# Cross-attention on one core: product 1 completed ahead of a sum, product 5's sums in another buffer, and the last batch's product 1 in seven blocks

## The chip, the core and the metric

The kernel runs on one core of a Trainium2 chip. A core has TensorE (PE in the profile, with its weight loads as PEld), VectorE (DVE), ScalarE (ACT), GpSimd (POOL) and SyncE (SP), which run their own instruction streams in order and wait for each other by semaphores; DMA queues are issued from SP and POOL. Matmuls read SBUF and write PSUM, which has eight banks of 512 fp32 columns on 128 partitions. The metric is the device time of one execution in microseconds (us).

## The reference

For each of 8 batches, x1 and x2 are 512 x 1024 (channels x positions), all in fp32:

```python
q = einsum('bcn,dc->bnd', x1, Wq) + bq          # d = 64
k = einsum('bcn,dc->bdn', x2, Wk) + bk[:, None]
v = einsum('bcn,dc->bdn', x2, Wv) + bv[:, None]
attn = softmax(einsum('bnd,bdm->bnm', q, k), axis=2)
out = einsum('bcm,bnm->bcn', v, attn) + x1
```

The kernel computes Y = x2 . attn^T first (512 x 1024 x 1024) and then Wv . Y (512 x 512 x 1024), adds bv and x1, and divides by the softmax's sums in between.

## The kernel before, in words

**Products.** Both large products are done by Winograd's form of Strassen's method: the left matrix, the right matrix and the result are cut into 2 x 2 quadrants, and seven products of quadrants (numbered 1 to 7 in the order in which the table MULT names them) with sums before and after replace eight. "S1" to "S4" are sums of left quadrants, "T1" to "T4" of right ones. The first stage (`first`, stage "y") makes Y from a quadrant of x2 (`s.a`) and of the exponentials (`s.t`); the second (`second`, stage "o") makes the result from Wv (`w`) and Y (`s.y`). Batches are called 0 to 7.

**Seven blocks inside a product.** Most products of the first stage, and some of the second, use the same method once more inside: `left_stream` and `right_stream` make the four left and the three right inner sums on DVE (L522; L537, L542, L544), and `multiply_seeded` runs seven blocks of 256 columns. A running sum ("chain") and one more ("third") sit in PSUM tiles of their own; ACT copies the chain into the quarters of the result's two banks between the steps (L651). The steps come in the order 1, 7, 6, 2, 5, 4, 3. `complete` adds the third part, kept in SBUF as v, to the second bank at the end, on DVE (L666). `multiply_57` (second stage, products 5 and 7) and `multiply_41` (first stage's product 4 interleaved with the second stage's product 1, "o1") are written out by hand. A product without inner blocks is `multiply` (L463), or `multiply_o1` (L483) for the second stage's product 1.

**Banks.** Two pairs of PSUM banks, a0 a1 and c0 c1, hold results; four more buffers are passed round (`ps_s`). In the last batch `o_bank` swaps the roles of a and c in the second stage.

**Order.** The order of all work is written out by hand in `period(s, n, nn, nnn)`: the first stage of batch s, the second stage of s, and between them the scores, maxima and exponentials of the next batch n, the queries and keys of the one after, and the loads. On each engine instructions run in the order in which this function issues them. `s.six` holds for batches 2 to 5, where product 6 has inner blocks too; `s.one` for batches 1 to 6, where product 1 of the second stage has (`five` in `period` means the same); n is None in the last batch.

**Around the change.** `sum_e` makes T1 and T2 (L340) and `sum_t3` has a POOL DMA add a quadrant to T3. `sums_5` are product 5's inner sums; the right ones stand in two buffers, in batches 2 to 5 "u5" and "u1". "u5" also holds, in the second stage, product 5's partial sums and then a block of the result (`uo`), to which a POOL DMA adds x1 and which an SP DMA then writes out. "aI3" holds product 2's inner left sums (batches 2 to 5), later product 3's. `total_1` sums the exponentials over a column: DVE folds (L283, L267), a partition reduction on POOL (L292), and a DMA that spreads one row over the partitions ("few", L294); `invert` takes the reciprocal (L300) and sends it to DRAM ("row", L302), `spread` brings it back on all partitions ("den", L307). `scale_y` multiplies a quadrant of Y with it (L755). `join_67` (L738), `evict_y`, `evict_t3` (L748) and `sum_y` (L427, L429) make the quadrants of Y and their sums.

**The last batch before.** Order after product 1: T1 and T2, complete 1, product 5's sums, product 7's left sums, product 2, then `total_1`, complete 2, y11, the first reciprocal, product 6, S4 (L108), product 7's right and 3's left sums, product 5, the second reciprocal, product 3's right sums, products 7 and 3, product 4's left sums, join, y22, product 4's right sums, product 4 (`multiply_seeded`, in the banks a0 a1), the scalings of y11, T3 and y22, T2 of Y, y21, T1, the scaling of y21, T4, and product 7's right sums of the second stage. The second stage then starts with product 1 as eight matmul instructions of 512 columns (an fp32 matmul shows as two), followed by 6, 2, 5 with 7 and 3, and 4 in `finish`.

Of the kernel before, what the change touches and what calls it, by code (L numbers as in the profile page):

```python
# [15 lines left out]
def kernel(  # L16
# [427 lines left out]
    def o_bank(s, bank):  # L444
        return {"a": "c", "c": "a"}.get(bank, bank) if s.b == B - 1 else bank

    def multiply(s, stage, i, left, right, n_k, hook=None, rows=range(2)):
# [4 lines left out]
        if stage == "o":  # L452
            bank = o_bank(s, bank)
            if i == 2:
                bank, opens = "c" if s.one else "p", False
        for j in rows:
            if opens:
# [20 lines left out]
    def multiply_o1(s):  # L478

        for j in range(2):  # L480
            s.bank["p", j] = ps = ps_s.tile([P, H], F32, tag="s", name=f"ps_o1{j}_{s.b}")
            for k in range(2):
                nc.tensor.matmul(  # L483
                    ps, w["11"][:, k, ts(j, P)], s.y["11"][:, k, :], start=k == 0, stop=False, skip_group_check=True
                )
# [39 lines left out]
    def inner_left(s, i, x, tag):  # L525
        weave(left_stream(s, i, x, tag))
# [105 lines left out]
    def multiply_seeded(s, i, v_tag, hooks={}, bank=None):  # L632
# [40 lines left out]
    )  # L673
    LAST41 = (
        (4, 1), (4, 7), (4, 6), (4, 2), ("o1", 7), ("o1", 1), (4, 5), ("o1", 6),
        ("o1", 2), ("o1", 4), ("o1", 5), (4, 4), ("o1", 3), (4, 3),
    )

    def multiply_41(s):

        s.inner["o1"] = inner_w["o1"]
        chain, third, *four = (
            ps_s.tile([P, H], F32, tag="s", name=f"ps_i4{k}_{s.b}") for k in ("chain", "third", "b0", "b1")
        )
        c, a = (
            [ps_a.tile([P, H], F32, tag=f"{k}{j}", name=f"ps_o{k}{j}_{s.b}_1") for j in range(2)] for k in "ca"
        )
        for j in range(2):
            s.bank["four", j], s.bank["c", j], s.bank["a", j] = four[j], c[j], a[j]
        v = sb.tile([P, 2, H], F32, tag="r", name=f"v41_{s.b}")  # L690
        v4, v1 = v[:, 0, left], v[:, 1, left]
        chain, third, copy = chain[:, left], third[:, left], nc.scalar.copy
        c0, c1, f0, f1 = ([x[:, left], x[:, right]] for x in (*c, *four))
        steps = {
            (4, 1): (chain, True, [(f0[0], chain)]),
            (4, 7): (third, True, [(v4, third)]),
            (4, 6): (chain, False, [(f1[0], chain)]),
            (4, 2): (f0[0], False, []),
            (4, 5): (chain, False, [(f0[1], chain)]),
            (4, 4): (f1[0], False, [(f1[1], chain)]),  # L700
            (4, 3): (f0[1], False, []),
# [12 lines left out]

        for i, z in LAST41 if s.b == B - 2 else ORDER41:
            ps, opens, copies = steps[i, z]
# [13 lines left out]
            if (i, z) == ("o1", 3):  # L730
# [3 lines left out]
                yield  # L734
        complete(four[1], v4)

# [51 lines left out]
    def evict_o(s, k, hook=None):  # L788


        bank, add = RESULT[k] if k != "11" else ("c" if s.one else "p", None)
        bank = o_bank(s, bank)
        r, h = int(k[0]) - 1, int(k[1]) - 1
# [208 lines left out]
    def period(s, n, nn, nnn):  # L1002
# [127 lines left out]
        else:  # L1130
            complete_1 = multiply_seeded(s, 1, "y11", {4: lambda: copied_s4(s)} if s.six else {})
            if s.b == 1:
                complete_1()
            early = s.b > 1 and n is not None
            sum_e(s, *(("T2",) if early else ("T1", "T2")))
            if s.b > 1:
                complete_1()
            sums_5 = (
                left_stream(s, 5, s.a["S1"], "i2"),
                right_stream(s, 5, s.t["T1"], "u5" if s.six else "y21", "u1"),  # L1140
            )
# [85 lines left out]
            if n is None:  # L1227
                inner_left(s, 4, s.a["22"], "a12")
            join_67(s)
# [44 lines left out]
        else:  # L1274
            if late:
                scale_y(s, "11", "T3", "22")
            sum_y(s, "T2")
# [5 lines left out]
        if five:  # L1283
# [5 lines left out]
            if nn is None:  # L1289
                first_sum()  # L1290
                begin_s1(n)
                end_s1(n)
        else:
            multiply_seeded(s, 4, "r", hooks, "c" if n else "a")()
        if n:
            load_a(n, "12")
        if nn:
            load_a(nn, "21", "22")
        evict_y(s, "21")
        if n is None:  # L1300
            sum_y(s, "T1")
        scale_y(s, "21")
        if five:
# [137 lines left out]
```

## Time and profile before

| what | value |
|---|---|
| median of 3 runs | 669.47 us (668.42 to 675.08) |
| the profiled execution's own time | 668.5 us |
| its span, first to last instruction | 666.7 us |
| TensorE busy | 661.5 us, 99% |
| VectorE busy | 617.5 us, 93% |
| ScalarE busy | 372.6 us, 56% |
| GpSimd busy | 225.2 us, 34% |
| granted TensorE clock | 1.0 throughout |
| DMA | 134.8 MB, mean 202 GB/s |

How rows are read: "500.46 3.60 PE L463 MATMUL out<-in ... x8 [0.15 <-DVE y]" in the order of time means start, duration of the merged instructions, engine, line, operation, tiles by name (buffer numbers left out), count, and the idle time of the engine before it with what ended it. In the groups a row has, behind the bar, busy time and mean duration in ns, then idle time. A wait's row has the total, the number and the longest. Consecutive records of one engine may overlap by 0.08 us (DVE) or more (PE), since an instruction starts while the one before still drains. The times of the trace are those of one execution: batch 1 begins at some 117 us, batch 7 at some 596 us, and one batch between takes 80 to 81 us.

### The profile page before, as it was taken

To read this page: it belongs to the slowest core of one execution; us is meant where nothing else is said; L and a number is where in the kernel's file an instruction comes from. 1 tells how busy PE (TensorE), PEld (TensorE's weight loads), DVE (VectorE), ACT (ScalarE), POOL (GpSimd) and SP (SyncE) were. 2 spreads that over 40 slices of the span, in tenths; PEclk is the share of its full clock that TensorE was granted. 3 is DMA by queue.
4 is the path that set the end of the run, shared out by engine and by line. 5 is a ranking of instruction groups with operands and counts; after the bars stand their busy time and mean duration, and the time that the engine had idled before them with its cause. 6 is when DMAs were issued, how large, how long until landed. Compare 5 with 4: busy or idle time off the path is not lost.

```text
span 666.7 us, 7925 instructions
## 1 busy us (share of the span) xinstructions
PE 661.5 (99%) x2618; PEld 431.0 (65%) x2618; DVE 617.5 (93%) x857; ACT 372.6 (56%) x706; POOL 225.2 (34%) x196
## 2 busy tenths in 40 slices
PE   9999999999999999999999999999999999999997
PEld 5434754757658666677666786576865757666864
DVE  0989999999999899998999899998999999998995
ACT  2755467446574564755756647656566455574321
POOL 0125315531255412553124531265214541244400
PEclk9999999999999999999999999999999999999999
DMA  9768677996899969999599995899947994399413
GB/s 307 276 206 296 147 232 139 187 233 220 240 182 220 241 175 283 172 228 245 158 278 186 256 236 152 247 203 234 269 91 171 209 278 132 74 179 250 90 42 125
DMA packets 51961, 134.81 MB, mean 202 GB/s; under 512 B 5712, under 2 KB 8272, under 8 KB 51920
## 3 DMA queue, kind: packets, MB, share of 16 engines
q0 software_dynamic: 24480, 61.94, 50.4%
q1 hardware_dynamic: 27152, 72.10, 30.4%
q8 instruction: 21, 0.34, 0.2%
q10 hardware_dynamic: 288, 0.26, 0.1%
q14 instruction: 20, 0.16, 0.1%
HBM read 86.77 MB, written 16.81 MB: 155 GB/s over the span
## 4 chain that ended last, share of the span: by engine, by line
PE 75%; DVE 16%; DMA 6%; issue 2%; ACT 0%; POOL 0%; ACTq 0%; DVEq 0%; SPq 0%; POOLq 0%
PE ps_yc L555 7%; PE ps_oc L463 6%; PE ps_ya L555 5%; PE ps_oa L598 5%; PE ps_s L237 5%; PE ps_ya L463 4%; PE ps_oa L463 4%; DMA out_dram<-uo 3%; PE ps_q L192 3%; PE ps_i5chain L555 3%; PE ps_i3chain L555 2%; PE ps_i7chain L555 2%; PE ps_k L192 2%; DVE max L257 2%; DMA uo<-in_x_dram 2%
## 5 line engine op out<-in xcount | busy, mean ns | idle before, releaser
L331 ACT ACTIVATE e<-e 128x1024 f32<-128x1024 f32 x60 | 63.4, 1058 | 30.0 <-DVE e L322 28.9
L292 POOL PARTITION_ALL_REDUCE den<-sum x16 | 52.8, 3298 | 69.6 <-DVE sum L267 64.7
L322 DVE TENSOR_TENSOR e<-e,top 128x1024 f32<-128x1024 f32 x60 | 72.6, 1218 | 2.0 <-POOL top L273 2.0
L273 POOL PARTITION_ALL_REDUCE top<-max x16 | 30.0, 1878 | 103.7 <-DVE max L267 85.2
L853 POOL DMA_DIRECT2D sum<-e x21 | 25.6, 1219 | 100.9 <-ACT e L331 45.7
L246 ACT COPY e<-ps_s 128x512 f32<-128x512 f32 x92 | 48.9, 619 | 9.6 <-PE ps_s L237 7.0
L237 PE MATMUL ps_s<-q,k 64*128 64x512 f32 (+1 forms) x192 | 48.0, 601 | 0.0
L257 DVE TENSOR_TENSOR max<-max,e 128x1024 f32<-128x1024 f32 x30 | 36.6, 1219 | 0.2
L237 PEld LDWEIGHTS ps_s<-q,k 64*128 64x128 f32 x192 | 17.4, 186 | 20.9 <-issue 17.4
L307 POOL DMA_DIRECT2D den<-row x16 | 8.9, 558 | 61.7 <-DMA row<-few 45.3
L755 DVE TENSOR_TENSOR y<-y,den 128x1024 f32<-128x1024 f32 x24 | 29.2, 1221 | 0.4
L463 PE MATMUL ps_oa<-yT,w_S 128*128 128x512 f32 x64 | 28.8, 593 | 0.0
L463 PE MATMUL ps_oc<-yT,w 128*128 128x512 f32 x64 | 28.8, 592 | 0.0
L651 ACT COPY ps_yc<-ps_i7chain 128x256 f32<-128x256 f32 x32 | 11.4, 357 | 30.2 <-PE ps_i7chain L555 24.2
L522 DVE TENSOR_TENSOR aI<-a,aI 128x256 f32<-128x256 f32 x60 | 25.2, 420 | 0.6
L522 DVE TENSOR_TENSOR aI<-a 128x256 f32<-128x256 f32 x60 | 25.8, 450 | 0.0
L192 PE MATMUL ps_q<-x_in_x_dram,wqk_sb 128*64 128x512 f32 x112 | 25.6, 598 | 0.0
L651 ACT COPY ps_ya<-ps_i5chain 128x256 f32<-128x256 f32 x32 | 11.4, 357 | 25.1 <-PE ps_i5chain L555 20.9
L340 DVE TENSOR_TENSOR eT<-eT,e 128x1024 f32<-128x1024 f32 (+1 forms) x18 | 24.0, 1365 | 0.1
L651 ACT COPY ps_ya<-ps_i1chain 128x256 f32<-128x256 f32 x28 | 10.0, 357 | 24.6 <-PE ps_i1chain L555 20.9
L555 PE MATMUL ps_yc<-e,aI 128*128 128x256 f32 x92 | 23.6, 379 | 0.0
L598 PE MATMUL ps_oa<-yT,w_S 128*128 128x512 f32 x48 | 23.5, 592 | 0.0
(322 smaller groups left out, 1826.3 us busy)
## 6 DMA issues: line engine op xcount, KB each, us to landing
x_in_x_dram<-in_x_dram SPq DMA_DIRECT2D x60, 512.0 KB, 8.1
a<-in_x2T_dram SPq DMA_DIRECT2D x32, 512.0 KB, 7.3
sum<-e POOLq DMA_DIRECT2D x21, 512.0 KB, 5.7
aS<-in_x2T_dram POOLq DMA_DIRECT2D x19, 512.0 KB, 9.6
eT<-eT POOLq DMA_DIRECT2D x16, 512.0 KB, 11.7
uo<-in_x_dram POOLq DMA_DIRECT2D x14, 512.0 KB, 10.9
r<-in_x_dram POOLq DMA_DIRECT2D x14, 512.0 KB, 8.8
e<-e POOLq DMA_DIRECT2D x14, 512.0 KB, 9.4
```

Source lines behind the costliest of these rows:

```text
L192: nc.tensor.matmul(ps[r, :], w_sb[:, c, :], s.x[:, c, ts(h, H)], start=(c == 0), stop=(c == CT - 1),)
L237: nc.tensor.matmul(ps[g][:, n], s.k[r, ts(i, P)], s.q[r, ts(h, H)][:, n], start=True, stop=True)
L246: nc.scalar.copy(e[:, g, i, :], ps[g])
L257: nc.vector.tensor_tensor(f, e[:, :, 0, :] if i == 1 else f, e[:, :, i, :], op)
L292: nc.gpsimd.partition_all_reduce(s.den[h], s.mx[h][:, 0, :], P, ReduceOp.add)
L322: nc.vector.tensor_tensor(e, e, top, ALU.subtract)
L331: nc.scalar.activation(e, e, AF.Exp)
L463: nc.tensor.matmul(ps, left[ka][:, k, ts(j, P)], right[kb][:, k, :], start=opens and k == 0, stop=i in (2, 3, 4) and k == n_k - 1, skip_gr ...
L522: nc.vector.tensor_tensor(v[k], v[x], v[y], op)
L555: nc.tensor.matmul(ps, s.inner[i][ka][:, k, :], s.inner[i, "t"][kb][:, k, :], start=opens and k == 0, stop=z in (2, 3, 4) and k == n_k - 1 ...
L598: nc.tensor.matmul(ps, w[ka][:, k, ts(j, P)], s.y[kb][:, k, :], start=False, stop=i == 3 and k == 1, skip_group_check=True,)
L651: nc.scalar.copy(out, of)
```

## The change

1. `complete_1()` stands ahead of `sum_e` in every batch from 1 on; before, only in batch 1 (in the others it came right behind T2, or T1 and T2).
2. The first of the two buffers for product 5's right inner sums is "aI3" in place of "u5" in batches 2 to 5.
3. In the last batch product 1 of the second stage is done in seven blocks too: `s.one` now holds there, `multiply_41` takes the place of `multiply_seeded(4)` and `multiply_o1`, with the banks swapped and an order of its own (ORDER41_7). There product 4 has no tiles for chain and third: the right half of its first bank serves as the chain, the left half takes step 7's result, which ACT copies to v before it copies the chain over it. y21 is evicted from those two tiles, and product 2's result from a0 a1.
4. In the last batch S4 and product 4's inner left sums are issued ahead of `total_1` and complete 2; the scaling of y11 and the three inner right sums of o1 stand ahead of the join, where product 4's left sums stood; y21 is scaled ahead of T1.

```diff
-            self.one = 1 <= b < B - 1
+            self.one = b >= 1
...
     def multiply_o1(s):
...
-            bank = o_bank(s, "a")
-            s.bank[bank, j] = a = ps_a.tile([P, H], F32, tag=f"{bank}{j}", name=f"ps_o{bank}{j}_{s.b}_1")
+            s.bank["a", j] = a = ps_a.tile([P, H], F32, tag=f"a{j}", name=f"ps_oa{j}_{s.b}_1")
...
+    ORDER41_7 = (
+        (4, 1), (4, 7), ("o1", 7), ("o1", 1), (4, 6), ("o1", 6), ("o1", 2),
+        (4, 2), (4, 5), ("o1", 4), ("o1", 5), (4, 4), ("o1", 3), (4, 3),
+    )
...
     def multiply_41(s):
...
+        last = s.b == B - 1
+        *inner, four0, four1 = (
+            ps_s.tile([P, H], F32, tag="s", name=f"ps_i4{k}_{s.b}")
+            for k in (() if last else ("chain", "third")) + ("b0", "b1")
+        )
+        to, grow = "ac" if last else "ca"
...
+        if last:
+            chain = f0[1]
+            steps = {
+                (4, 1): (chain, True, []),
+                (4, 7): (f0[0], False, [(v4, f0[0]), (f0[0], chain)]),
+                (4, 5): (chain, False, [(f1[1], chain)]),
+                (4, 4): (f1[0], False, []),
+            }
...
-        if k == "22" or s.b == B - 1 and k == "21":
+        if k == "22":
             bank, add = "a", 6
...
     def period(s, n, nn, nnn):
...
             complete_1 = multiply_seeded(s, 1, "y11", {4: lambda: copied_s4(s)} if s.six else {})
-            if s.b == 1:
-                complete_1()
             early = s.b > 1 and n is not None
+            complete_1()
             sum_e(s, *(("T2",) if early else ("T1", "T2")))
-            if s.b > 1:
-                complete_1()
             sums_5 = (
                 left_stream(s, 5, s.a["S1"], "i2"),
-                right_stream(s, 5, s.t["T1"], "u5" if s.six else "y21", "u1"),
+                right_stream(s, 5, s.t["T1"], "aI3" if s.six else "y21", "u1"),
             )
...
             if n is None:
                 copy_t4(s)
                 add_t4(s)
+                sum_a(s, "S4")
+                inner_left(s, 4, s.a["22"], "a12")
             if s.b > 1:
                 total_1(s)
             complete_2()
...
-                sum_a(s, "S4")
+                if n:
+                    sum_a(s, "S4")
...
             complete_3 = multiply_seeded(s, 3, "r", hooks, "c")
             if n is None:
-                inner_left(s, 4, s.a["22"], "a12")
+                scale_y(s, "11")
+                inner_right(s, "o1", s.y["11"], "i2")
             join_67(s)
...
-                scale_y(s, "11", "T3", "22")
+                scale_y(s, "T3", "22")
...
+        elif late:
+            weave(multiply_41(s))
         else:
-            multiply_seeded(s, 4, "r", hooks, "c" if n else "a")()
+            multiply_seeded(s, 4, "r", hooks)()
...
         evict_y(s, "21")
+        scale_y(s, "21")
         if n is None:
             sum_y(s, "T1")
-        scale_y(s, "21")
...
-        if not five:
+        if s.b == 0:
             second(1)
```

More of the change, by code (lines that the diff above doesn't have):

```diff
@@ L444, in o_bank @@
     def o_bank(s, bank):
[L445 removed]
+        return {"a": "c", "c": "a"}[bank] if s.b == B - 1 else bank
     def multiply(s, stage, i, left, right, n_k, hook=None, rows=range(2)):
@@ L692, in multiply_41 @@
[L692 to L696, printed above, removed]
+            s.bank["four", j], s.bank[to, j], s.bank[grow, j] = (four0, four1)[j], c[j], a[j]
+        if last:
+            v = sb.tile([P, H], F32, tag="top", name=f"v41_{s.b}", bufs=2)
+        else:
+            v = sb.tile([P, 2, H], F32, tag="r", name=f"v41_{s.b}")[:, 0]
@@ new lines, in multiply_41 @@
+        v4, v1, copy = v[:, left], v[:, right], nc.scalar.copy
+        c0, c1, f0, f1 = ([x[:, left], x[:, right]] for x in (*c, four0, four1))
+        if last:
+            chain = f0[1]
[5 more added lines that the diff above has]
+            }
+        else:
+            chain, third = inner[0][:, left], inner[1][:, left]
+            steps = {
+                (4, 1): (chain, True, [(f0[0], chain)]),
+                (4, 7): (third, True, [(v4, third)]),
+                (4, 5): (chain, False, [(f0[1], chain)]),
+                (4, 4): (f1[0], False, [(f1[1], chain)]),
+            }
```

22 lines of the change are left out of this document (9 added, 13 removed).

## The prediction

> **What bounds the kernel now.** I read the profile's page first, then who TensorE waits for, then its order of time, and last the queues that feed it.
>
> ```profile
> PE 661.5 (99%) x2618; PEld 431.0 (65%) x2618; DVE 617.5 (93%) x857; ACT 372.6 (56%) x706; POOL 225.2 (34%) x196
> PE ps_oc L463 <- DVE y L755: 0.2, 1, 0.2
> 633.33 1.03 PE L555 MATMUL ps_i4chain<-eT,a 128*128 128x256 f32 x4
> 634.19 1.03 PE L555 MATMUL ps_i4third<-eI4eT,aI 128*128 128x256 f32 x4
> 639.37 3.60 PE L483 MATMUL ps_o<-y,w 128*128 128x512 f32 x8
> 642.81 1.02 PE L463 MATMUL ps_oc<-yT,w_S 128*128 128x512 f32 x2
> ```
>
> The first row is the page's; the reader sees one engine without a pause and VectorE (DVE) close behind. The next is one of four rows of TensorE's waits, of which only the warm-up's is longer. Records of matmuls overlap, so their cost is read from start to start: four instructions of 256 columns take 634.19 - 633.33 = 0.86 us, 0.215 each; eight of 512 columns take 642.81 - 639.37 = 3.44 us, 0.43 each. The stream of matmuls is the time, and a change is worth what it takes out of this stream or tears into it. DVE idles little, and it decides where the tears are.
>
> **A. Product 1's third part ahead of T2 (batches 2 to 7).** The order on DVE changes, not the work.
>
> ```profile
> 446.10 3.23 POOL L292 PARTITION_ALL_REDUCE den<-sum  x1 [3.51 <-DVE sum L267]
> 447.24 3.31 DVE L340 TENSOR_TENSOR eT<-eT,e 128x1024 f32<-128x1024 f32 x2
> 450.48 0.69 DVE L666 TENSOR_TENSOR ps_ya<-ps_ya,v 128x512 f32<-128x512 f32 x1
> 605.22 2.35 DVE L340 TENSOR_TENSOR eT<-eT,e 128x1024 f32<-128x1024 f32 x2
> 617.36 3.23 POOL L292 PARTITION_ALL_REDUCE den<-sum  x1 [5.51 <-DVE sum L267]
> 617.77 1.28 DVE L771 TENSOR_TENSOR y<-ps_yc,uy 128x512 f32<-128x512 f32 x2
> 619.05 1.62 DVE L108 TENSOR_TENSOR aS<-a,aS 128x1024 f32<-128x1024 f32 x1
> ```
>
> Two sums of 128x1024 take 2.35 us alone, but 3.31 when they start 1.14 us into a partition reduction on POOL: 0.96 lost. S4, begun 1.69 us into one, takes 1.62 instead of about 1.2: 0.4 lost. Both fit one reading: from some point on, a DVE sum of two SBUF tiles can't begin until 2.1 us after the reduction's start. The eviction of y, which reads PSUM and one SBUF tile, runs inside the same stretch in its usual 1.28. Completing product 1 is of that second kind (PSUM and v). Put first, it fills 0.60 us (451.08, the next start, less 450.48) of a pause that T2 has anyway; T2 ends when it ended, and all of DVE's work behind it starts 0.60 us earlier. If completing is held up too, the order costs and brings nothing. I take 0.60.
>
> The Trainium skill, "SBUF — State Buffer", "Who interferes with whom", says that a DVE instruction with two SBUF inputs contends with a GpSimd one that reads SBUF, and one with at most one SBUF input doesn't; the trace agrees in the 3.31 against the 1.28. Were it not so, A's share would fall out of the sum below. The same section has the loser blocked for the other's whole instruction, where these rows show a release at 2.1 of 3.23 us; the measurement decides.
>
> The completion now waits for the copy of step 4. In the last batch:
>
> ```profile
> 601.60 0.36 ACT L651 COPY ps_ya<-ps_i1chain 128x256 f32<-128x256 f32 x1 [0.51 <-PE ps_ya L555]
> 601.98 3.32 DVE L340 TENSOR_TENSOR eT<-e,e 128x1024 f32<-128x1024 f32 x2
> ```
>
> The copy ends at 601.96, DVE comes at 601.98: no wait to speak of. Behind a wait there T2, the inner sums and product 6's operands would queue.
>
> What 0.60 us are worth to TensorE:
>
> ```profile
> L555 PE MATMUL ps_i6chain<-eI6y,aI 128*128 128x256 f32 x16 | 4.4, 398 | 0.0
> L555 PE MATMUL ps_i6chain<-eI6yT,aI 128*128 128x256 f32 x16 | 4.1, 379 | 0.0
> 292.54 0.41 DVE L522 TENSOR_TENSOR aI<-aS,aI 128x256 f32<-128x256 f32 x1
> 293.06 0.73 PEld L555 LDWEIGHTS ps_i6chain<-eI6y,aI 128*128 128x128 f32 x4 [0.27 <-ACT ps_ya L651]
> 293.09 1.10 PE L555 MATMUL ps_i6chain<-eI6y,aI 128*128 128x256 f32 x4
> ```
>
> Sixteen matmuls of product 6's step 6 (four batches) cover 4.4 us, sixteen of step 5 4.1: about 0.07 us a batch, 1.10 instead of 1.03. The named releaser is a copy; but the left sum ends at 292.95 and the weights load 0.11 later, so DVE is the late one. Half a microsecond earlier removes it: **-0.28**.
>
> **B. Product 5's first sums in another buffer (batches 2 to 5).**
>
> ```profile
> DVE eI5u L537 <- DMA out_dram<-uo: 9.0, 4, 2.8
> 454.20 9.45 DMA out_dram<-uo
> 500.46 3.60 PE L463 MATMUL ps_oa<-yT,w_S 128*128 128x512 f32 x8
> 499.27 0.69 DVE L713 TENSOR_TENSOR ps_oc<-ps_oc,v 128x512 f32<-128x512 f32 x1
> 500.00 0.57 ACT L733 COPY ps_oa<-ps_oc 128x512 f32<-128x512 f32 x1 [0.49 <-DVE ps_oc L713]
> 502.93 1.23 DVE L755 TENSOR_TENSOR y<-y,den 128x1024 f32<-128x1024 f32 x1
> 504.21 1.98 PE L463 MATMUL ps_oc<-y,w 128*128 128x512 f32 x4 [0.15 <-DVE y L755]
> ```
>
> Four times DVE waits for the DMA that writes the last batch's result out of u5, 9.0 us in all. The buffer aI3 is free then: product 2 has finished with it, and its next user, product 3's left sums, comes on DVE after product 5's completion, which needs later steps than the sums in aI3. So no wait takes this one's place at once. Mostly the 9.0 us are DVE's own, not TensorE's. Only batch 5 pays: the chain runs over DVE from that DMA to 504.21. Late DVE completes product 1 of the result late (499.27), ACT's copies queue behind it, product 4 and the scaling of y21 follow, and TensorE starts at 504.21 instead of 500.46 + 3.44 = 503.90; its first four also cover 1.98 instead of 3 x 0.43 + 0.59 = 1.88. Together **-0.41**, and nothing if DVE meets another wait on that way; I take the whole, since 2.8 us are freed and 0.4 needed.
>
> **C. Last batch, product 1 of the result in seven blocks.** Eight matmuls of 512 columns become fourteen of 256: 14 x 0.215 = 3.01 for 3.44, **-0.43**. Four small copies come on ACT, which idles there; one completion of 0.6 us on DVE replaces part of the 1.2 of scaling y11, which moves ahead.
>
> Product 4 now uses the right half of its own first bank as the running sum, so its step 6 waits for two copies after step 7 (ACT, L729), with only two one-row blocks (0.86 us) between.
>
> ```profile
> 635.26 0.37 ACT L651 COPY v<-ps_i4third 128x256 f32<-128x256 f32 x1 [0.51 <-PE ps_i4third L555]
> 571.00 0.36 ACT L729 COPY ps_oc<-ps_oc 128x256 f32<-128x256 f32 x1 [1.31 <-PE ps_oc L720]
> 571.27 0.38 ACT L729 COPY v<-ps_oc 128x256 f32<-128x256 f32 x1
> 568.11 1.13 PE L720 MATMUL ps_i4chain<-eI4eT,aI 128*128 128x256 f32 x4
> ```
>
> Step 7's copy starts at 635.26, a second 0.27 to 0.37 later, and it ends at 635.89 to 635.99; TensorE is there at 635.92, and a torn stream adds 0.10 (1.13 for 1.03). So 0.1 to 0.2; I take **+0.18**.
>
> **D. Last batch, S4 and the sums moved.** S4 and product 4's four left sums (0.75 + 0.88) go ahead of the second column sum. Scaling y11 (1.22) and its three inner sums (0.69 + 0.41 + 0.41 by the rows of their shapes above) stand where the left sums stood.
>
> ```profile
> 628.24 0.75 DVE L522 TENSOR_TENSOR aI<-a 128x256 f32<-128x256 f32 x2
> 612.56 0.88 DVE L522 TENSOR_TENSOR aI<-a,aI 128x256 f32<-128x256 f32 x2
> 615.31 1.23 DVE L283 TENSOR_TENSOR sum<-e 128x1024 f32<-128x1024 f32 x1 [1.86 <-DMA e<-e]
> 626.62 0.36 ACT L651 COPY ps_yc<-ps_i7chain 128x256 f32<-128x256 f32 x1 [0.51 <-PE ps_yc L555]
> 623.96 0.54 POOL L307 DMA_DIRECT2D den<-row  x1 [1.93 <-DMA row<-few]
> DMA to landing us min/median/max: 3.5/3.5/3.5
> 630.17 1.23 DVE L738 TENSOR_TENSOR uy<-uy,uy 128x1024 f32<-128x1024 f32 x1 [0.26 <-ACT uy L743]
> 632.64 1.22 DVE L537 TENSOR_TENSOR eI4eT<-eT 128x1024 f32<-128x1024 f32 x1
> ```
>
> DVE idles 1.86 us ahead of the column sum. With A it arrives there at 612.8 (612.56 + 0.88 - 0.60); S4 (1.14, no reduction beside it) and the left sums (1.6) end at about 615.5, so the column sum is 0.2 us late; without A, 0.8. What hangs on it is a queue: POOL's reduction, the DMA few and, behind them in order, the DMAs that spread the FIRST denominators. Those land at 623.96 + 3.5 = 627.5 now, and nobody wants them until product 4's sums (632.64) are long done; afterwards they land at 627.7, and scaling y11 wants them at 627.6: product 7's last copy ends at 626.98, and its completion takes 0.60. From 627.75 the scaling, inner sums (2.7), the join and y22 (2.47) bring product 4's first right sum to 632.95, and its end, with 1.22, to 634.2. TensorE wants it at 634.19 and needs some 0.1 after a sum's end. **+0.25** (0 to 1.0, the upper end for a sum 0.8 late plus the 0.10), since that lies nearest to the rows with A. After that DVE has 1.22 less to do, and y21 is scaled ahead of T1: I see no wait up to the end.
>
> **Sum:** -0.28 - 0.41 - 0.43 + 0.18 + 0.25 = -0.69 us against the profiled execution's 668.5 us (span 666.7): 667.8. The median of the runs shown is 669.47, 0.97 above that execution, with runs from 668.42 to 675.08; I add 0.4 for such scatter: **668.2 us**.
>
> **Rivals.** *The freed DVE time reaches nobody.* B's wait goes, but the stall of batch 5 stays, as another wait takes its place on the way to 499.27. For it: one lateness of 40 us is rarely one wait's alone; against it: the earlier batches idle before the same completion and pay nothing. -0.28 - 0.43 + 0.43 = -0.28: 668.2, with the scatter 668.6. Chance 0.17.
>
> *Slower: the first denominators land late.* If completing product 1 is held by the reduction like T2, A brings nothing, the column sum of the last batch is 0.8 us late, and scaling y11 blocks DVE ahead of join, y22 and product 4's right sums; TensorE pays one for one from 634.19 on. 0 - 0.41 - 0.43 + 0.18 + 0.95 = +0.29: 668.8, with the scatter 669.2 to 669.8. It turns the sign once the scaling is some 0.9 us later than 627.6 and A's share is gone. For it: a slack of over 5 us becomes none. Against it: y's evictions run beside a reduction undisturbed. Chance 0.18.
>
> *It does all it says and nothing else* (D free, as C's wait): -1.0, 667.5. Chance 0.10; my forecast 0.50. The last 0.05 are for something unseen.
>
> **Range and chances.** The forecast alone covers 667.5 to 669.0. With the free case and its run-to-run tenths the range begins at 667.0; it ends at 670.2, the late denominators at their upper bound (D at 1.0) with the median's 0.97 on top. A measurement here can tell about 1%, 6.7 us, from no change; no case comes near it: same 0.95, faster 0.02, slower 0.03.
>
> **What would show it.** In the changed kernel: no DVE wait for out_dram<-uo; step 6 of product 6 at 1.03; second(2) of batch 5 right behind second(6); L666 of product 1 ahead of L340 at 0.69, T2 ending as before. In the last batch fourteen matmuls of 0.215 for L483's eight, a small PE gap at (4,7), another at (4,6), and the scaling of y11 starting just after the den DMA lands. I am wrong if DVE, not TensorE, has idle time taken from it that turns up as PE gaps elsewhere, or if the sums placed ahead push the column sum back by a microsecond.

## The result, and the profile after

The changed kernel takes 668.01 us (median of 22 runs, 667.31 to 668.49) against 669.16 us for the kernel before in the same comparison (22 runs, 668.42 to 675.08). The ratio is 0.9976, with a 95% interval of 0.9967 to 0.9986; on a second chip it was 0.9977 (0.9968 to 0.9986; 667.74 against 669.44 us). That is no change by the prediction's bound of 1% and a small gain by the interval. Some executions of most kernels here take about 6 us more (the one of them that was profiled, in e2, spent 87.79 us in batch 1, at a granted clock of 0.994 over the execution), which widens several intervals below; there I go by the lengths of the batches.

The page of the changed kernel, its busy times and its chain of work that ended last:

```profile
PE 661.0 (99%) x2624; PEld 432.1 (65%) x2624; DVE 614.8 (92%) x861; ACT 373.4 (56%) x709; POOL 224.9 (34%) x196
PE 97%; DMA 2%; DVE 1%; issue 0%; ACT 0%; ACTq 0%; DVEq 0%
```

The busy times hardly move. The chain does: it runs over TensorE for 97% of the span; before, it was 75%, with DVE 16% and DMA 6%. Who waits for whom, TensorE's rows first, then DVE's (total, times, longest):

```profile
PE ps_ya L464 <- ACT e L317: 0.2, 1, 0.2
```

```profile
DVE ps_ya L666 <- ACT ps_ya L651: 7.7, 7, 1.5
```

TensorE's wait for y21 is gone, and so is the wait of DVE for out_dram<-uo (9.0 us). DVE's largest wait behind the first batch's is now product 5's completion waiting for ScalarE's copies, that is, for TensorE's steps: DVE is ahead.

The length of each batch, from TensorE's first matmul of product 1 to the next batch's (the last one to the start of its last matmul), in us, from the trace of each kernel's profiled execution:

| kernel | 1 | 2 | 3 | 4 | 5 | 6 | 7 |
|---|---|---|---|---|---|---|---|
| before | 81.17 | 80.67 | 80.48 | 80.47 | 80.90 | 75.15 | 66.57 |
| after | 81.16 | 80.53 | 80.35 | 80.34 | 80.35 | 75.15 | 66.48 |
| after, second chip | 81.17 | 80.53 | 80.34 | 80.35 | 80.34 | 75.16 | 66.48 |
| e1 order alone | 81.17 | 80.87 | 80.34 | 80.69 | 81.83 | 76.04 | 66.70 |
| e2 buffer alone | 87.79 | 80.68 | 80.47 | 80.48 | 80.47 | 75.16 | 66.80 |
| e3 last batch alone | 81.17 | 80.78 | 80.47 | 80.66 | 81.54 | 75.15 | 67.38 |
| e4 sums back | 81.17 | 80.53 | 80.35 | 80.34 | 80.35 | 75.15 | 68.58 |
| e8 late sum | 81.17 | 80.52 | 80.35 | 80.34 | 80.35 | 75.41 | 69.81 |
| e6 own tiles | 81.17 | 80.53 | 80.34 | 80.35 | 80.35 | 75.15 | 66.19 |
| e7 other order in 6 | 81.17 | 80.54 | 80.35 | 80.34 | 80.35 | 74.87 | 66.56 |
| e9 own chain | 81.17 | 80.54 | 80.34 | 80.35 | 80.34 | 75.15 | 66.31 |
| e10 the same, other order in 6 | 81.16 | 80.53 | 80.35 | 80.34 | 80.35 | 74.87 | 66.24 |
| e11 old buffer | 81.17 | 80.53 | 80.34 | 80.35 | 80.95 | 75.15 | 66.61 |

From batch 1 on the changed kernel's execution is 1.04 us shorter than that of before (span less the start of batch 1: 549.34 and 548.30): 0.52 in the four batches' 0.13, another 0.42 in batch 5, and 0.09 in batch 7. Its head, up to batch 1, was 0.53 longer: TensorE's wait for the load of x_head ended at 12.06 us, in before's execution at 11.54, and from there on both heads take the same time (105.85 and 105.84). Batch 5 in order of time:

```profile
440.29 1.03 PE L555 MATMUL ps_i1chain<-e,a 128*128 128x256 f32 x4
446.22 3.23 POOL L292 PARTITION_ALL_REDUCE den<-sum  x1 [3.51 <-DVE sum L267]
447.36 0.69 DVE L666 TENSOR_TENSOR ps_ya<-ps_ya,v 128x512 f32<-128x512 f32 x1
447.95 2.71 DVE L340 TENSOR_TENSOR eT<-eT,e 128x1024 f32<-128x1024 f32 x2
450.59 0.41 DVE L522 TENSOR_TENSOR aI<-aS 128x256 f32<-128x256 f32 x1
454.11 1.03 PE L555 MATMUL ps_i6chain<-eI6y,aI 128*128 128x256 f32 x4
460.34 1.22 DVE L537 TENSOR_TENSOR eI5aI<-eT 128x1024 f32<-128x1024 f32 x1
500.45 3.60 PE L464 MATMUL ps_oa<-yT,w_S 128*128 128x512 f32 x8
503.88 1.45 PE L464 MATMUL ps_oc<-y,w 128*128 128x512 f32 x3
```

L666 takes its 0.69 beside the reduction, T2 behind it still ends 4.4 us after the reduction's start (447.95 + 2.71 - 446.22; before 447.24 + 3.31 - 446.10 = 4.45), and the first left sum comes 10.30 us after product 1's start (before 451.08 - 440.17 = 10.91). Step 6 of product 6 runs untorn at 1.03. Product 5's first sum starts at 460.34 without a wait, and the second stage passes from product 6 to 2 at 503.88, 3.43 after 500.45, in the stream's own rhythm. The last batch:

```profile
614.95 1.22 DVE L283 TENSOR_TENSOR sum<-e 128x1024 f32<-128x1024 f32 x1
623.59 0.54 POOL L307 DMA_DIRECT2D den<-row  x1 [1.92 <-DMA row<-few]
627.16 1.22 DVE L776 TENSOR_TENSOR y<-y,den 128x1024 f32<-128x1024 f32 x1
632.40 1.21 DVE L537 TENSOR_TENSOR eI4eT<-eT 128x1024 f32<-128x1024 f32 x1
633.74 1.06 PE L741 MATMUL ps_i4b<-eI4eT,aI 128*128 128x256 f32 x4
634.84 0.37 ACT L750 COPY v<-ps_i4b 128x256 f32<-128x256 f32 x1 [2.27 <-PE ps_i4b L741]
635.24 0.36 ACT L750 COPY ps_i4b<-ps_i4b 128x256 f32<-128x256 f32 x1
635.65 1.13 PE L741 MATMUL ps_i4b<-eI4eT,aI 128*128 128x256 f32 x4
642.23 1.94 PE L464 MATMUL ps_oc<-yT,w_S 128*128 128x512 f32 x4
```

The column sum starts as soon as S4 and the left sums are done, without the 1.86 us of idling ahead of it; the scaling of y11 has its denominators in time; product 4's first right sum ends at 633.61, and (4,7) follows at 633.74 with 0.03 lost (1.06 for 1.03). What costs here are the two copies in a row: (4,6) could start at 635.50 (635.28 for the last matmul ahead of it, and 0.215), and starts at 635.65.

### The profile page after: what moved, and what is told of

Its sections match the earlier page's. It is cut to its first block, busy times and chain, and to the rows that moved or that the text cites. A ratio compares the mean times of both kernels' runs of the same rounds, so it can differ in the third digit from the quotient of the medians.

```text
span 666.2 us, 7951 instructions
## 1 busy us (share of the span) xinstructions
PE 661.0 (99%) x2624; PEld 432.1 (65%) x2624; DVE 614.8 (92%) x861; ACT 373.4 (56%) x709; POOL 224.9 (34%) x196
## 4 chain that ended last, share of the span: by engine, by line
PE 97%; DMA 2%; DVE 1%; issue 0%; ACT 0%; ACTq 0%; DVEq 0%
PE ps_yc L555 9%; PE ps_oc L464 8%; PE ps_ya L555 7%; PE ps_s L237 6%; PE ps_oa L598 6%; PE ps_oa L464 5%; PE ps_ya L464 4%; PE ps_q L192 4%; PE ps_i5chain L555 3%; PE ps_i4b L741 3%; PE ps_k L192 3%; PE ps_i3chain L555 3%; PE ps_i7chain L555 3%; PE ps_oc L741 3%; PE ps_i1chain L555 3%; PE ps_i2chain L555 3%
## 5 line engine op out<-in xcount | busy, mean ns | idle before, releaser
L841 POOL DMA_DIRECT2D r<-in_x_dram x14 | 23.2, 1660 | 0.8 <-issue 0.8
```

## The experiments

**e1, the order alone** (kernel before with part A only).

```diff
-            if s.b == 1:
-                complete_1()
             early = s.b > 1 and n is not None
+            complete_1()
             sum_e(s, *(("T2",) if early else ("T1", "T2")))
-            if s.b > 1:
-                complete_1()
```

> The kernel before, with product 1 completed ahead of T2 in batches 2 to 7 and nothing else. Theory (the completion fits into a pause that the partition reduction makes anyway, so DVE is 0.6 us ahead): step 6 of product 6 starts without a gap in batches 2 to 5, each of these batches 0.13 us shorter from product 1 to product 1 as in the changed kernel, about -0.5 us in all; the gap of 0.42 us in batch 5 ahead of y21's product stays. Rival (the late sums come from DVE's wait for the output DMA): the step 6 gaps stay, no change of the time.

Measured: 668.74 us (12 runs) against 669.50, ratio 1.0 (0.9975 to 1.0025): undecided. Batch 3 is 0.14 shorter and step 6 of product 6 is untorn in all of batches 2 to 5. But batches 2, 4 and 5 are longer than before, by 0.2, 0.2 and 0.9. Its order of time in batch 5, then a row of batch 6, and last the row of the DMA issues of batch 5's place (KB, us to landing):

```profile
440.10 1.03 PE L555 MATMUL ps_i1chain<-e,a 128*128 128x256 f32 x4
464.61 1.23 DVE L537 TENSOR_TENSOR eI5u<-eT 128x1024 f32<-128x1024 f32 x1 [4.37 <-DMA out_dram<-uo]
505.07 2.41 PE L463 MATMUL ps_oc<-y,w 128*128 128x512 f32 x5 [0.21 <-DVE y L755]
559.94 1.23 DVE L755 TENSOR_TENSOR y<-y,den 128x1024 f32<-128x1024 f32 x1 [1.19 <-DMA den<-row]
```

```profile
out_dram<-uo SPq DMA_DIRECT2D x1, 512.0 KB, 10.5
```

In this execution the write of uo took 10.5 us to land, in that of before 9.45. DVE starts product 5's first sum 24.51 us after the batch's start (464.61 - 440.10), before 23.57 (463.74 - 440.17), and TensorE waits for y21 behind it. The 0.94 is the whole of the difference (81.83 - 80.90 = 0.93). Batch 6 is 0.89 longer as well (76.04): there another landing is late, that of the denominators, for which DVE waits 1.19 us ahead of the first scaling (0.12 in before), and TensorE waits for the scaled quadrant. So A does its work, and late landings take it away and more. This put B's price in question, which I had read from one execution.

**e2, the buffer alone** (kernel before with part B only).

```diff
-                right_stream(s, 5, s.t["T1"], "u5" if s.six else "y21", "u1"),
+                right_stream(s, 5, s.t["T1"], "aI3" if s.six else "y21", "u1"),
```

> The kernel before, with product 5's first right sums in aI3 and nothing else. Theory: DVE no longer waits for the output DMA in batches 2 to 5 (9.0 us gone), TensorE gains only the 0.42 us of batch 5; the step 6 gaps stay, 0.13 us a batch. Total -0.4 us. Rival: the step 6 gaps go too, -0.9 us in all.

Measured: 669.06 us against 669.50, ratio 1.0009 (0.9981 to 1.0037): undecided. Batch 5 has lost 0.43 (80.47) and is like 3 and 4; step 6 stays torn, as its row in batch 5 shows:

```profile
461.23 1.10 PE L555 MATMUL ps_i6chain<-eI6y,aI 128*128 128x256 f32 x4
```

So the tear is A's to remove and not a consequence of the wait for the DMA. With B in place A's 0.13 comes on top (80.47 here, 80.35 in the changed kernel). Without B a batch that waits for the landing gains nothing from A: by the table under e11 its length follows from the landing, with A and without.

**e3, the last batch alone** (the changed kernel with A and B undone).

```diff
+            if s.b == 1:
+                complete_1()
             early = s.b > 1 and n is not None
-            complete_1()
             sum_e(s, *(("T2",) if early else ("T1", "T2")))
+            if s.b > 1:
+                complete_1()
...
-                right_stream(s, 5, s.t["T1"], "aI3" if s.six else "y21", "u1"),
+                right_stream(s, 5, s.t["T1"], "u5" if s.six else "y21", "u1"),
```

> The changed kernel with the old order of product 1's completion and the old buffer: only the last batch's part is left. Theory (first denominators queued behind the column sum): DVE comes 0.6 to 0.8 us later to the column sum than in the changed kernel, the first denominators land as much later, scaling y11 waits for them, and TensorE has a gap of 0.4 to 0.8 us at product 4's step 7; batch 7 is 0.3 to 0.6 us longer than before, the total +0.3 to +0.6 us. Rival (the moved sums hide anyway): batch 7 0.1 us shorter, total -0.1 us.

Measured: 670.15 us, ratio 1.0012 (0.9990 to 1.0035). Batch 7 takes 67.38, 0.90 more than in the changed kernel; B has no part in that batch, and DVE comes into it as in the changed kernel's execution (4.23 and 4.21 us after its start, by the eviction of the last result block), so this is what A is worth there beside C and D. In order of time:

```profile
628.86 1.23 DVE L776 TENSOR_TENSOR y<-y,den 128x1024 f32<-128x1024 f32 x1 [0.59 <-DMA den<-row]
635.37 1.13 PE L741 MATMUL ps_i4b<-eI4eT,aI 128*128 128x256 f32 x4 [0.66 <-DVE eI4eT L537]
```

This is my slower rival, seen: the scaling of y11 waits 0.59 for the first denominators, and TensorE has its gap at (4,7).

**e4, S4 and the left sums back** (the changed kernel without that move of part D).

```diff
-                sum_a(s, "S4")
-                inner_left(s, 4, s.a["22"], "a12")
             if s.b > 1:
                 total_1(s)
...
-                if n:
-                    sum_a(s, "S4")
+                sum_a(s, "S4")
...
             complete_3 = multiply_seeded(s, 3, "r", hooks, "c")
             if n is None:
+                inner_left(s, 4, s.a["22"], "a12")
                 scale_y(s, "11")
```

> The changed kernel with S4 and product 4's left sums back in their old places; the scaling of y11 and o1's sums stay ahead of the join. Theory: DVE pays scaling, o1's sums and left sums in one stretch, 1.67 us more ahead of product 4's right sums; step 7 of product 4 starts 1.3 to 1.7 us late, +1.3 to +1.7 us on the changed kernel (about +0.3 on the one before). Rival (DVE has the slack there): no gap, the changed kernel's time.

Measured: 670.77 us, ratio 1.0028 (1.0001 to 1.0055); batch 7 is 68.58, +2.10, more than the 1.3 to 1.7 expected.

```profile
614.91 1.22 DVE L283 TENSOR_TENSOR sum<-e 128x1024 f32<-128x1024 f32 x1 [2.37 <-DMA e<-e]
635.95 1.13 PE L741 MATMUL ps_i4b<-eI4eT,aI 128*128 128x256 f32 x4 [1.86 <-DVE eI4eT L537]
```

Without the move DVE idles 2.37 us ahead of the column sum, and the 2.9 us of sums stand where they are in the way. The move turns that idling into work; without it part C would cost more than it takes out.

**e8, the column sum late** (the changed kernel; in the last batch `total_1` behind y11).

```diff
-            if s.b > 1:
+            if s.b > 1 and n:
                 total_1(s)
             complete_2()
             evict_y(s, "11")
+            if n is None:
+                total_1(s)
```

> The changed kernel with the last batch's second column sum behind y11 in place of ahead of product 2's completion: 1.8 us later, no work added. Theory: the spread of the first denominators queues behind it on POOL, lands 1.8 us later, scaling y11 waits for it 1.6 us and TensorE has a gap of 1.5 to 1.8 us at product 4's step 7; +1.5 to +1.8 us on the changed kernel. Rival (the scaling finds its denominators anyway, or DVE catches up before product 4): no gap.

Measured: 672.43 us, ratio 1.0046 (1.0014 to 1.0077); batch 7 is 69.81, +3.33, more than I had expected.

```profile
619.84 1.19 DVE L537 TENSOR_TENSOR eI7yT<-e 128x1024 f32<-128x1024 f32 x1
619.93 4.20 POOL L292 PARTITION_ALL_REDUCE den<-sum  x1 [8.08 <-DVE few L300]
631.22 1.23 DVE L776 TENSOR_TENSOR y<-y,den 128x1024 f32<-128x1024 f32 x1 [1.38 <-DMA den<-row]
```

The reduction starts 2.20 us later in the batch (619.93 - 596.53 against 616.99 - 595.79); 0.4 of this is DVE's later arrival in the batch in this execution (4.62 us after its start for 4.21). It also takes 4.20 in place of 3.23: a DVE sum of two SBUF tiles had begun 0.09 us ahead of it, and the trains of e5 show the same lengthening. The scaling starts 3.32 us later in the batch (631.22 - 596.53 against 627.16 - 595.79), and TensorE is later by just that: the first denominators are one for one on the path, once they are late.

**e5, sums beside a reduction** (trains of twelve small DVE instructions, each run with and without a partition reduction beside it; nothing of the kernel's computation is left).

```diff
+        def two(k):
+            nc.vector.tensor_tensor(o[:, k, :], x[:, 0:Q], y[:, 0:Q], ALU.add)
+        def mixed(k):
+            nc.vector.tensor_tensor(o[:, k, :], ps[:, 0:Q], y[:, 0:Q], ALU.add)
+        def one(k):
+            nc.vector.reciprocal(o[:, k, :], x[:, 0:Q])
```

> Leaves the whole computation out: trains of twelve short DVE instructions (128x256) right behind the start of a partition reduction on POOL, and the same without one; inputs two SBUF tiles, PSUM and SBUF, or one SBUF tile; then sums of 128x1024 at three distances from the start. Theory: two SBUF inputs are held until 2.1 us after the start of an adding reduction (of 3.2) and 0.9 us after that of a maximum (of 1.8), then run at their usual 0.42; PSUM and SBUF, and one SBUF input, aren't touched. Rival (held for the reduction's whole instruction): the first sum starts when the reduction ends, 3.2 us. Second rival (all DVE work is slowed alike): the PSUM train is longer too.

The order of time, pairs without and with the reduction (two SBUF tiles, PSUM and one tile, the reduction for maxima, large sums), and then the first line's min/median/max in ns:

```profile
102.61 4.11 DVE L87 TENSOR_TENSOR o<-x,y 128x256 f32<-128x256 f32 x12
107.70 6.15 DVE L87 TENSOR_TENSOR o<-x,y 128x256 f32<-128x256 f32 x12
107.95 3.26 POOL L98 PARTITION_ALL_REDUCE red<-src  x1 [7.54 <-DVE src L96]
29.04 4.06 DVE L90 TENSOR_TENSOR o<-ps,y 128x256 f32<-128x256 f32 x12
34.07 4.06 DVE L90 TENSOR_TENSOR o<-ps,y 128x256 f32<-128x256 f32 x12
34.33 3.23 POOL L98 PARTITION_ALL_REDUCE red<-src  x1 [8.91 <-DVE src L96]
79.90 4.95 DVE L87 TENSOR_TENSOR o<-x,y 128x256 f32<-128x256 f32 x12
80.15 1.81 POOL L98 PARTITION_ALL_REDUCE red<-src  x1 [17.16 <-DVE src L96]
85.83 4.40 DVE L106 TENSOR_TENSOR big<-x,y 128x1024 f32<-128x1024 f32 x2
86.08 4.06 POOL L98 PARTITION_ALL_REDUCE red<-src  x1 [4.12 <-DVE src L96]
```

```profile
L87 DVE TENSOR_TENSOR o<-x,y x72: 409/413/2464, 16.8 to 170.2; 128x256 f32<-128x256 f32 x72
```

A sum of two SBUF tiles loses 2.04 us once per reduction (6.15 for 4.11): one instruction of 2.46 in place of 0.41. It is the second of its train, 0.34 (4.11 / 12) after 107.70, held from 108.04 for 2.05, that is, until about 2.14 us after the reduction's start. Two large sums begun 0.42 and 1.08 us into a reduction take 4.04 and 3.38 us in place of the 2.35 that they take alone, which puts the release at 2.11 both times. Sums that read PSUM and one SBUF tile lose nothing (4.06 both times), nor do twelve reciprocals of one SBUF tile (19.47 both times). This is the release point that the prediction read out of two rows, and the reason why a completion fits into the pause and T2 doesn't. The Trainium skill, "SBUF — State Buffer", "Who interferes with whom", has the loser blocked for the whole instruction; here it is let go after about two thirds of it, and the measurement decides.

**e11, the old buffer in the changed kernel** (B undone), run with the changed kernel on one chip.

```diff
-                right_stream(s, 5, s.t["T1"], "aI3" if s.six else "y21", "u1"),
+                right_stream(s, 5, s.t["T1"], "u5" if s.six else "y21", "u1"),
```

> The changed kernel with the first sums of product 5's right operand back in the old buffer, so that they wait for the writing out of uo again. Theory: that write takes 9.2 to 10.5 us to land, other in each batch and each execution, so the buffer costs more than the 0.41 us that the profile of before showed in batch 5: one to four of the batches 2 to 5 are 0.1 to 1.0 us longer than 80.35, in the sum 0.6 to 2.5 us, and the median is 0.4 to 1.5 us above the changed kernel's, with a wider scatter. Rival: only batch 5 is touched, by 0.4 us as in before; the other batches stay at 80.35 to 80.53, and the median is 0.3 to 0.5 us above.

Measured: 669.10 us (11 runs, 668.22 to 670.03), ratio 0.9996 (0.9987 to 1.0005), against 667.74 (11 runs, 667.48 to 668.59) for the changed kernel, whose interval lies below. So B is worth 1.36 us in the median with A in place, of 1.70 in all there. The profiled execution of e11 was its fastest (668.22), and in it, of the batches that use u5, only batch 5 is long (the last row is batch 7's (4,7), for later):

```profile
439.82 1.03 PE L555 MATMUL ps_i1chain<-e,a 128*128 128x256 f32 x4
463.45 1.23 DVE L537 TENSOR_TENSOR eI5u<-eT 128x1024 f32<-128x1024 f32 x1 [3.50 <-DMA out_dram<-uo]
633.92 1.13 PE L741 MATMUL ps_i4b<-eI4eT,aI 128*128 128x256 f32 x4
```

With this the cases of the four kernels that still use u5 can be laid side by side: the start of the sum in u5 after the batch's first matmul, read from such rows, against the batch's length.

| execution, batch | sum in u5 starts after | batch takes | difference |
|---|---|---|---|
| e1, 4 | 23.37 | 80.69 | 57.32 |
| e3, 2 | 23.46 | 80.78 | 57.32 |
| e1, 2 | 23.55 | 80.87 | 57.32 |
| before, 5 | 23.57 | 80.90 | 57.33 |
| e11, 5 | 23.63 | 80.95 | 57.32 |
| e3, 5 | 24.22 | 81.54 | 57.32 |
| e1, 5 | 24.51 | 81.83 | 57.32 |

From that sum on the way to the next batch takes 57.32 us in all of them, with A and without (e3's batch 4, at 23.34, takes 80.66 and fits too). Where the landing is earlier (before, batch 3: 22.61; e1, batch 3: 22.96) the batch keeps its 80.35 to 80.48. With A the limit is 80.35 - 57.32 = 23.03 us (23.21 in batch 2, which takes 80.53), and each tenth behind it is a tenth on the clock, in any of four batches. Summed over batches 2 to 5 and set against the same batches without u5, the four profiled draws cost 0.43 us (before), 0.60 (e11), 1.36 (e3) and 2.16 (e1). In the changed kernel's own batch 5 the write of uo, issued at 454.32, took 10.3 us, some 24.3 after the batch's start; in u5 that would have cost 1.3 us. Its batch takes 80.35.

**e6 and e7, what the shared tile costs.** e6 gives product 4 of the last batch tiles of its own for chain and third, as in the other batches, and their order of blocks; e7 also moves (o1,7) and (o1,1) ahead of (4,2) in batch 6. These two versions don't sum all of the last batch's product 4 and are read for their time alone; the instructions are otherwise the same.

```diff
-            for k in (() if last else ("chain", "third")) + ("b0", "b1")
+            for k in ("chain", "third", "b0", "b1")
...
-        for i, z in (ORDER41_6, ORDER41_7)[s.b - B + 2] if s.b >= B - 2 else ORDER41:
+        for i, z in ORDER41_6 if s.b == B - 2 else ORDER41:
```

> The changed kernel with the last batch's product 4 in the form of the other batches: running sum and third part in tiles of their own, order ORDER41. Theory: the gap ahead of step 6 (0.15 and 0.10 us) and the 0.06 ahead of product 6 of the result come from sharing a bank with the running sum and from copies late in the order; without them batch 7 is 0.2 to 0.3 us shorter than in the changed kernel. Rival: the gap moves to another copy of that order, no change.

> As the one with own tiles, and batch 6 with another order of the fourteen blocks (o1's 7 and 1 ahead of product 4's step 2, o1's 6 and 4 each behind a long block). Theory: two of batch 6's three gaps (0.14 and 0.28 us) are TensorE waiting for ACT's copies of o1; 0.3 us less in batch 6. Rival: c0 and c1 aren't free yet when o1 starts (the eviction of T3 reads them), and a gap of like size comes there.

Measured: e6 667.81 us, 0.9976 (0.9953 to 1.0000), batch 7 at 66.19, -0.29. e7 668.02 us, 0.9979 (0.9953 to 1.0004): batch 6 at 74.87, -0.28 as expected, but batch 7 at 66.56, +0.37 on e6. The order of time of e7:

```profile
627.95 1.23 DVE L767 TENSOR_TENSOR y<-y,den 128x1024 f32<-128x1024 f32 x1 [0.35 <-DMA den<-row]
646.05 1.12 PE L464 MATMUL ps_oa<-y,w 128*128 128x512 f32 x2 [0.16 <-DVE y L767]
```

DVE waited 0.35 us for the first denominators, and TensorE for y21 at the end. What batch 6 gave, batch 7 took back in that execution; that it would in others is not shown.

**e9 and e10, a whole computation with an own chain.** e9 is the changed kernel with one more tile for the chain and the third part in the right half of the result's first tile; e10 adds e7's order in batch 6.

```diff
-            chain = f0[1]
+            chain = inner[0][:, left]
             steps = {
-                (4, 1): (chain, True, []),
-                (4, 7): (f0[0], False, [(v4, f0[0]), (f0[0], chain)]),
-                (4, 5): (chain, False, [(f1[1], chain)]),
-                (4, 4): (f1[0], False, []),
+                (4, 1): (chain, True, [(f0[0], chain)]),
+                (4, 7): (f0[1], False, [(v4, f0[1])]),
+                (4, 5): (chain, False, [(f0[1], chain)]),
+                (4, 4): (f1[0], False, [(f1[1], chain)]),
             }
...
-        for i, z in (ORDER41_6, ORDER41_7)[s.b - B + 2] if s.b >= B - 2 else ORDER41:
+        for i, z in ORDER41_6 if s.b == B - 2 else ORDER41:
```

> The changed kernel once more, on the chip of the three that follow, as their yardstick. Expected: 0.9967 to 0.9986 of the kernel before, as in the first comparison; batches 2 to 5 at 80.35 to 80.53 us, batch 6 at 75.15, batch 7 at 66.4 to 66.6.

> The changed kernel, but in the last batch product 1 of the inner pair's seven blocks sums its chain in a PSUM tile of its own, the third part (4,7) goes to the right half of the result's first tile, and the blocks stand in the order of the middle batches, with (o1,7) and (o1,1) between (4,1) and (4,7). The computation is whole. Theory: (4,6) then waits for no chain of two copies, so the gap of 0.26 us at (4,6) and the 0.06 us ahead of the result's product 6 go: batch 7 takes 66.1 to 66.3 us against 66.48, and the time is 0.2 to 0.4 us under the changed kernel's. Rival: VectorE carries the end of this batch anyway and TensorE meets the lost 0.3 us again at y22: batch 7 stays at 66.4 to 66.6 us.

> The kernel with the own chain tile, and in batch 6 the blocks (o1,7) and (o1,1) moved ahead of (4,2). The computation is whole. Theory: the waits of TensorE in batch 6 shrink (batch 6 at 74.87 us against 75.15), and what VectorE has to spare in batch 7, the 0.13 and 0.31 us that it waited for ScalarE's copies, takes up the earlier start: batch 7 at 66.2 to 66.3 us, 0.5 to 0.6 us under the changed kernel in all. Rival: from the middle of batch 6 on VectorE has nothing to spare, or the first denominators land behind it, as in the run with the other order before (0.35 us of waiting): batch 7 at 66.4 to 66.6 us, and 0.2 to 0.3 us under the changed kernel in all.

Measured: e9 667.48 us (7 runs), 0.9972 (0.9961 to 0.9983); e10 667.56 us (8 runs), 0.9971 (0.9961 to 0.9981); the changed kernel beside them 667.74, 0.9977 (0.9968 to 0.9986). Batch 7 is 66.31 in e9, 0.17 of the 0.32 expected:

```profile
635.39 1.03 PE L741 MATMUL ps_i4chain<-eI4eT,aI 128*128 128x256 f32 x4
642.03 0.70 DVE L734 TENSOR_TENSOR ps_i4b<-ps_i4b,v 128x512 f32<-128x512 f32 x1 [0.91 <-ACT ps_i4b L750]
644.09 1.22 DVE L776 TENSOR_TENSOR y<-y,den 128x1024 f32<-128x1024 f32 x1
645.36 2.84 PE L464 MATMUL ps_oa<-y,w 128*128 128x512 f32 x6
```

(4,6) starts untorn at 635.39, but DVE then idles 0.91 us for a ScalarE copy, scales y21 until 645.31, and TensorE meets the rest there. In this execution DVE also came into the batch 0.27 us later than in the changed kernel's (4.48 for 4.21 after its start). e10 keeps batch 6's 0.28 this time (74.87, and 66.24 in batch 7): the scaling of y11 waited 0.04 us for its denominators, in e7 0.35. By batch lengths e10 is 0.52 us under the changed kernel; by time the intervals overlap, so that either beats the changed kernel is not shown. Both beat the kernel before.

## Why the prediction was right, point by point

The forecast was 668.2 us; it came to 668.01, inside the range. The mechanisms of A, B and D are those that the runs show, but the number is nearer than the terms are. The sum of the parts was -0.69 and measured -1.04 in the profiled executions, and I put 0.4 on top for a scatter that the changed kernel's median does not have over its profiled execution. Both misses made the forecast too high, by 0.75 us together. Most of that is hidden by the head, which I took as fixed: in the changed kernel's profiled execution it was 0.53 us longer, by first loads that landed later. That is luck.

The start of batch 7 on DVE, before's two rows first:

```profile
600.66 1.41 DVE L814 SCALAR_TENSOR_TENSOR o<-ps_oc,bv_sb,uo 128x512 f32<-128x512 f32 x2
608.09 0.41 DVE L522 TENSOR_TENSOR aI<-aS 128x256 f32<-128x256 f32 x1
600.00 1.40 DVE L836 SCALAR_TENSOR_TENSOR o<-ps_oc,bv_sb,uo 128x512 f32<-128x512 f32 x2
601.56 0.70 DVE L666 TENSOR_TENSOR ps_ya<-ps_ya,v 128x512 f32<-128x512 f32 x1 [0.15 <-ACT ps_ya L651]
606.83 0.41 DVE L522 TENSOR_TENSOR aI<-aS 128x256 f32<-128x256 f32 x1
```

From the eviction of the last result block to the first left sum DVE takes 608.09 - 600.66 = 7.43 us before and 606.83 - 600.00 = 6.83 after: A's 0.60. DVE is ahead by another 0.23 there that is not A's. It came into the batch earlier, 4.21 us after its start (600.00 - 595.79) for 4.44 (600.66 - 596.22), and so even waited 0.15 for the copy of step 4, a wait that the prediction had at nothing. This arrival is a draw: it lies between 4.21 and 4.62 in the thirteen executions, and with it goes the wait for the denominators' landing in batch 6 (none in the changed kernel's execution, 0.12 in before's, 1.19 in e1's).

- **A**, -0.28 predicted, **-0.52** measured (0.13 in each of batches 2 to 5). The mechanism is right (e1, e2, e5): the completion fits the pause, T2 ends as before. The term was mis-sized: I counted the tear, 1.10 for 1.03, and not the gap in front of the torn matmul, another 0.06. In the last batch A gives the 0.60 that I took (6.83 for 7.43, above), and it keeps the slower rival away: 0.90 by e3.
- **B**, -0.41 predicted. In the two profiled executions it is 0.42 beside A's share, in the median **1.36** (e11 against the changed kernel), and 0.43 to 2.16 in the four draws that were profiled. The step that failed is "Only batch 5 pays": it held for the one execution I had. The landing scatters, each of four batches pays what lies behind its limit, and the execution profiled, at 668.5, was 0.7 to 1.1 faster than the medians. That the earlier batches idle and pay nothing was luck of that draw, and so is the 0.42. The rival in which the freed time reaches nobody is refuted by batch 5's 80.35 and by e2.
- **C**, -0.43 + 0.18. The fourteen short matmuls run at 0.215. The wait at (4,6) cost 0.15 with 0.105 for the tear, 0.26, and product 6 behind it 0.06 that I had not counted.
- **D**, +0.25 predicted, **0.03** measured in the changed kernel's execution. The mechanism, the first denominators queued behind the column sum, is the one that decides (e3, e4, e8). The small number is a draw: as DVE had come into the batch 0.23 us earlier than in before, the column sum starts only 0.07 us later in it (614.95 - 595.79 = 19.16; before 615.31 - 596.22 = 19.09), not 0.2, and (4,7) is on time. In e11, whose batch 7 has the same code, DVE arrives at 4.42, the column sum starts at 19.37, 0.28 later than before, (4,7) is torn (1.13), and the batch takes 66.61, 0.13 more.
- **C and D together.** -0.43 + 0.26 + 0.06 + 0.03 = -0.08, against 0.09 measured in batch 7 between the two executions. But batch 7 differs by more than that with the same code (before's 66.57 and e2's 66.80; the changed kernel's 66.48 and e11's 66.61), and no run leaves out the last batch's part alone. So what the change brings in batch 7 lies between nothing and 0.3 us; a closer figure is not shown.
- **The scatter**, +0.4, was wrong in kind. The changed kernel's median (668.01) is its profiled execution's time (667.98). What I took for noise of the machine was in good part the wait of B in its other draws, as e11's median beside its own profiled execution suggests (669.10 and 668.22).
- **The slower rival** exists as described: e3 has it at 0.90 for the 0.95 that I had priced.
- **Sums.** The terms of the free case add up to -1.12, not to -1.0 (667.4), and those of the late denominators at their upper bound, with A's share gone and 0.97 on top, to 669.8, not to 670.2. Neither changes how the forecast came out.

What stays open: e1 and e2 don't tell by time what A and B are worth alone. Of the scatter of before two more sources can be seen and were not tried: the denominators' landing in batch 6 and the first loads (TensorE's wait for x_head ends between 10.92 and 12.09 us in the thirteen executions). The four executions with u5 have the four shortest heads (116.83 to 117.43; the others 117.56 to 118.52); whether that is chance is not known.

## What to carry to other kernels

A wait for a DMA's landing that one profiled execution shows as nearly hidden is one draw: look at the landing in every repetition of the loop, find from which landing on it reaches the end (here one constant, 57.32 us), and price the wait by the spread of landings and not by the one seen. A DVE operation that reads PSUM and one SBUF tile can be put into the pause that a partition reduction on GpSimd makes for sums of two SBUF tiles. Parts of a change can depend on each other: here the new blocks in the last batch bring little, and without the earlier completion or the moved sums they cost 0.90 or 2.10 us.

## What the runs showed of the hardware

- A partition reduction of 3.23 us holds a DVE sum of two SBUF tiles until about 2.1 us after its start; the reduction for maxima, 1.81 us, costs such a train 0.84 (4.95 for 4.11).
- It works the other way too: where a large DVE sum of two SBUF tiles was already running, the reduction took 4.06 in the probe and 4.20 in e8 in place of 3.23.
- A write of 512 KB of the same form took 9.45, 10.3 and 10.5 us from issue to landing at the same place of three executions (batch 5 of before, the changed kernel and e1).
- A TensorE stream that is interrupted loses more than the interruption: four matmuls of 256 columns cover 1.13 us in place of 1.03 behind a gap of 0.15 and more, and 1.10 behind one of 0.06 (step 6 of product 6 before).
